# A selective scan beside two other layers: delta's product ahead of the spread and softplus ahead of the decay in the fifth slot

## Chip, cores and metric

The kernel runs on one core of a Trainium2 chip, in one launch. The metric is the device time of that core in microseconds. Before the change it is 28012.72 us, the median of three runs (28011.66 to 28014.21).

The core has five engines that run beside each other and meet through semaphores: TensorE (PE in the profile, with its weight loads shown as PEld), VectorE (DVE), ScalarE (ACT), GpSimd (POOL) and SyncE (SP), which here only issues DMAs. Each has its own queue of instructions.

## What is computed

x has 16 images of 192 channels and 64 x 64 pixels. Four layers follow each other, each added to its input. Each normalises its input by groups of channels first (`_gn`). Layer 0 is a small network per channel, with softplus weights and tanh, of which the kernel does much on TensorE and ScalarE. Layer 1 is a shift in five directions with a product over channels. Layer 2, the scan, is the one that the change is in. Layer 3 is a sum of four depthwise convolutions, a product over channels and a batch norm. Layer 2, cut to what matters (K = 4 directions, N = 16 states, R = 6):

```python
xs = jnp.stack([xf, xt, xf[..., ::-1], xt[..., ::-1]], axis=1)
x_dbl = jnp.einsum('bkdl,kcd->bkcl', xs, x_proj_weight)
dts, Bs, Cs = jnp.split(x_dbl, [R, R + N], axis=2)
dts = jnp.einsum('bkrl,kdr->bkdl', dts, dt_projs_weight)
delta = jax.nn.softplus(dts + dt_projs_bias[None, :, :, None])
A = -jnp.exp(A_logs.astype(jnp.float32)).reshape(K, D, N)
def step(h, inp):
    d, u, Bt, Ct = inp
    dA = jnp.exp(d[..., None] * A)
    h = dA * h + (d * u)[..., None] * Bt[:, :, None, :]
    y = jnp.einsum('bkdn,bkn->bkd', h, Ct)
    return (h, y)
```

The recurrence runs along the 4096 pixels, for each direction, channel and state by itself.

## The kernel before

Two images of 192 channels make 384 rows, that is three tiles of 128 partitions (`NT` = 3); there are 8 such pairs. For each pair `pair` runs `scans` (layer 2) and then `layer3`. Beside the scans of one pair `scans` does the front of the next pair, layers 0 and 1, the projections of layer 2 and their rearrangement: a generator `fr`, of which a little is taken in every step. The front of the first pair runs alone ahead of all, and the last pair's scans have no front beside them.

The scans of a pair are 48 turns (`todo`, index `t`): 3 row tiles, by 4 directions in `ORDER` (1, 3, 0, 2), by 4 stretches of 1024 pixels. A turn has 16 steps, one for each state `n`; `s` counts the steps of a pair. Steps and turns are numbered from 0 here, so the fifth slot of the change is step 4. All engines are given their instructions in program order (`_Engines(tc, True)`), so the loop in `scans` is the order of every queue. A step of the loop issues, in this order:

- SP: the load of C for step s + 2 (`load_c`, two or one of 512 or 256 KB broadcast over partitions); in steps 2, 4 and 6 the loads of later turns' `bp`, `dt` and `xc`.
- VectorE: `product(s)`, du times B in the PSUM tile `pbt`, and `scan(s)`, the recurrence, into an `h` tile in SBUF.
- ScalarE: in `scan(s)`, the copy of the last column of h into `state` for the next turn.
- GpSimd: in `scan(s)`, h times C, in place; in every fourth step (n % 4 == 1) also a DMA that adds the h of the step before to this one.
- ScalarE: `decay(s + 3)`, exp of delta times A into `dA`, preceded by a table load where the active table is another one.
- TensorE: `spread(s + 2)`, which copies row n of B to all partitions of a `pbt` tile (2 matmuls of 512 columns).
- In step 4, the first part of `step_rest(t + 1)`: on TensorE delta's product `v` for the next turn (two halves, four matmul instructions in the trace), on ScalarE softplus of v into `delta`, with a load of the softplus table before. The generator's second part follows in step 8: on GpSimd du = delta times x.
- In all steps but step 5, a share of `fr` (layer 0 keeps step 5 free too): matmuls `p` and tanh, sigmoid or copies on ScalarE for layer 0, matmuls `l_p` for layer 1.
- TensorE: `add_up(s - LATE)`, `LATE` = 4, which adds h to the PSUM tile `ysum` (not for n % 4 == 0); in step 3, ahead of the share of `fr`. Step 3 adds the last h of the turn before and ScalarE copies ysum out to `X` or `Xt`. Step 5 starts this turn's ysum: a turn of direction 0 begins it with eight matmuls, of directions 2 and 3 with four, of direction 1 with none, ahead of the four for h.

`v` and `ysum` share one PSUM buffer (pool `py`, one buffer, one tag). So v waits for the copy of the turn before (step 3), and ysum of step 5 waits for softplus to have read v. `pbt` has two buffers (pool `pb`): the spread of step s + 2 waits for scan s. `dA` has three, `h` eight, `state` is read in the next turn of the same direction. Which buffer of a pool a tile gets is decided when the program is built, by the planner's own estimate of what will be free first, not by rotation alone.

In the profile, all instructions of the scans and of the front beside them have the line of the recording helper, L64; they are told apart by their tiles. `softplus` and `exp` lie in different activation tables (`SOFTPLUS`, `TANH`); layer 0's tanh runs from the exp table or the sigmoid one.

Of the kernel before, what the change touches and what calls it, by code (L numbers as in the profile page):

```python
# [104 lines left out]
def conv_preact_kernel(ctx: ExitStack, tc: tile.TileContext, a: dict):  # L105
# [206 lines left out]
    def image(ap):  # L312
        return ap.rearrange("p (h w) -> p h w", w=HW)
# [468 lines left out]
    def scans(i, o, st3, nxt):  # L782

        E = _Engines(tc, True)
        with ExitStack() as es:
# [22 lines left out]
            T = len(todo)  # L808
# [4 lines left out]
            def seq(t, k, at, n):  # L813


                v = image(t) if k % 2 == 0 else columns(t)
                return v[:, at // HW : (at + n) // HW, :]

            def load_bp(t):
                if t < T:  # L820
                    j, k, at, first = todo[t]
                    bps[t] = two.tile([BP, LC], BF16, name="bp")
                    E.sp.dma_start(out=bps[t], in_=o.bp[k, :, at : at + LC])

            def load_dt(t):
                if t < T:
                    j, k, at, first = todo[t]
                    dts[t] = one.tile([32 + RD, 512], F32, name="dt")
                    src, r = (o.dtp, RD * (k // 2)) if k % 2 else (o.dt, RD * (2 + k // 2))
                    for h in range(2):  # L830
                        E.sp.dma_start(
                            out=dts[t][32 * h : 32 * h + RD, :],
                            in_=src[r : r + RD, at + 512 * h : at + 512 * h + 512],
                        )

            def load_xn(j):
                if j < NT:
                    xns[j] = one.tile([P, L], F32, name="xn")
                    E.sp.dma_start(out=xns[j], in_=row_tiles(o.x2)[:, j, :])

            def norm_xn(j):
                if j < NT:
                    normalise(E.dve, xns[j], xns[j], o.gm, o.rstd, j)

            def load_xc(t):
                if t < T and todo[t][1] == 0:
                    j, k, at, first = todo[t]
                    xcs[t] = one.tile([P, LC], F32, name="xc")
                    E.sp.dma_start(out=xcs[t], in_=row_tiles(o.x2)[:, j, at : at + LC])

            def load_c(s):
                t, n = divmod(s, N)
                j, k, at, first = todo[t]
                cb = cbs[s] = cp.tile([P, LC], F32, name="cb")
                src, row = (o.c, 64 + 16 * k) if k % 2 == 0 else (o.cp, 16 * (k - 1))
                for b, rows in {
                    0: ((0, slice(0, P)),),
                    1: ((0, slice(0, 64)), (1, slice(64, P))),
                    2: ((1, slice(0, P)),),
                }[j]:  # L860
                    r = row + N * b + n
                    E.sp.dma_start(
                        out=cb[rows, :],
                        in_=src[r : r + 1, at : at + LC].to_broadcast([rows.stop - rows.start, LC]),
                    )

            def step_rest(t):


                j, k, at, first = todo[t]  # L870
                dt = dts.pop(t)
                v = py.tile([P, LC], F32, name="v", tag="ysum")
                for h in range(2):
                    rows = slice(32 * h, 32 * h + RD)
                    E.pe.matmul(
                        v[:, 512 * h : 512 * h + 512],
                        dtw[rows, k, j, :],
                        dt[rows, :],
                        start=True,
                        stop=True,  # L880
                    )
                delta = two.tile([P, LC], F32, name="delta")
                E.table(SOFTPLUS)
                E.act.activation(delta, v, AF.Softplus, bias=dtb[:, k, j : j + 1])
                yield
                du = two.tile([P, LC], F32, name="du")
                E.gps.tensor_tensor(image(du), image(delta), seq(xns[j], k, at, LC), ALU.mult)
                made[t] = delta, du

            def decay(s):  # L890
                t, n = divmod(s, N)
                j, k, at, first = todo[t]
                dA = dAs[s] = da.tile([P, LC], F32, name="dA")
                E.table(TANH)
                E.act.activation(dA, made[t][0], AF.Exp, scale=a_neg[:, k, j, n : n + 1])

            def spread(s):
                t, n = divmod(s, N)
                j, k, at, first = todo[t]
                pbt = pbs[s] = pb.tile([P, LC], F32, name="pbt")  # L900
                w = [
                    pick[:, n : n + 1].to_broadcast([BP, P]),
                    pick_mix[:, n, :, :].rearrange("p a b -> p (a b)"),
                    pick[:, N + n : N + n + 1].to_broadcast([BP, P]),
                ][j]
                for c in range(LC // 512):
                    cs = slice(512 * c, 512 * c + 512)
                    E.pe.matmul(pbt[:, cs], w, bps[t][:, cs], start=True, stop=True)

            def product(s):  # L910
                E.dve.tensor_tensor(pbs[s], made[s // N][1], pbs[s], ALU.mult)

            def scan(s):
                t, n = divmod(s, N)
                j, k, at, first = todo[t]
                if (j, k) not in state:
                    state[j, k] = sp_.tile([P, N], F32, name="state")
                dA, pbt, cb = dAs.pop(s), pbs.pop(s), cbs.pop(s)
                back = k >= 2
                flip = slice(None, None, -1) if back else slice(None)  # L920
                h = hs[s] = hp.tile([P, LC], F32, name="h")
                v = state[j, k][:, n : n + 1]
                E.dve.tensor_tensor_scan(
                    h[:, flip], dA[:, flip], pbt[:, flip], 0.0 if first else v, ALU.mult, ALU.add
                )
                E.act.copy(v, h[:, 0:1] if back else h[:, LC - 1 : LC])
                E.gps.tensor_tensor(h, h, cb, ALU.mult)
                if n % 4 == 1:
                    E.gps.dma_start(out=h, in_=hs[s - 1], accum_op=ALU.add)
# [69 lines left out]
            gstep = iter(())  # L999
            for s in range(total):  # L1000
                t, n = divmod(s, N)
                j, k, at, first = todo[t]
                if s + 2 < total:
                    load_c(s + 2)
                if n == 2:
                    load_bp(t + 1)
                if n == 4:
                    load_dt(t + 2)
                if n == 6:
                    load_xc(t + 1)  # L1010
                product(s)
                E.between()
                scan(s)
                if s + 3 < total:
                    decay(s + 3)
                if s + 2 < total:
                    spread(s + 2)
                if (t + 2) % (K * NC_) == 0 and n == 14:
                    load_xn(j + 1)
                if (t + 1) % (K * NC_) == 0 and n == 5:  # L1020
                    norm_xn(j + 1)
                if n > 4:
                    next(fin, None)


                if n == 3:
                    add_up(s - LATE)
                    if s >= LATE and (s - LATE + 1) % (K * NC_ * N) == 0:
                        fin = finish(j - 1)
                elif n == 4:  # L1030
                    gstep = step_rest(t + 1) if t + 1 < T else iter(())
                    next(gstep, None)
                elif n == 8:
                    next(gstep, None)

                if kind == "l0":
                    for _ in range({5: 0}.get(n, 1)):
                        kind = next(fr, None) if kind == "l0" else kind
                elif n != 5:
                    done = 0  # L1040
                    while done < (1.99 if n in (0, 8, 12) else 0.99) and kind != "l0":
                        kind = next(fr, 1)
                        done += kind if isinstance(kind, float) else 1
                if n != 3:
                    add_up(s - LATE)
# [293 lines left out]
```

## Time and profile before

| what | value |
| --- | --- |
| median of three runs | 28012.72 us |
| the profiled execution's own time | 28007.89 us |
| its span | 28006.0 us |
| scans of the first pair | 1210 to 4172 us of the span |
| scans of the last pair | 24486 to 27270 us |
| between two pairs' scans (layer 3) | about 366 us |
| mean granted TensorE clock | 0.912 |

The span runs from the first to the last instruction; 1.9 us of the execution's time lie around it. Within the scans of the first pair, three stages follow each other by what the front does: layer 0 (about 1480 to 2880 us), layer 1 (to about 3500 us) and the projections with their rearrangement, then nothing. Busy time in these stages:

| us of the span | length | PE | DVE | ACT | POOL |
| --- | --- | --- | --- | --- | --- |
| 1210 to 1480 | 270 | 214.70 | 258.73 | 178.60 | 203.94 |
| 2880 to 3500 | 620 | 564.50 | 581.78 | 241.50 | 504.58 |
| 3500 to 4170 | 670 | 497.56 | 609.22 | 338.66 | 490.03 |
| 24486 to 27270 (last pair) | 2784 | 1927.16 | 2667.69 | 1171.76 | 2118.85 |

How to read the lines below: a row of the groups gives the line, the engine, the operation, what it writes and reads, how often, the busy time and mean nanoseconds, and the idle time just before with what ended it. A row of waits gives who waited for whom, with the sum, the number and the longest. In the timeline, the bracket gives the engine's idle time before the instruction and what ended it.

### The profile page before, as it was taken

What the parts mean: (1) busy time and instruction counts of PE and PEld (TensorE: products, weight loads), DVE (VectorE), ACT (ScalarE), POOL (GpSimd) and SP (SyncE); (2) the same over time, 40 slices, a digit from 0 to 9 for tenths busy, and PEclk for the clock granted to TensorE, in tenths of its full rate; (3) what the DMA queues carried; (4) which work ended last, traced back from release to release, by engine and by line L of the source; (5) the groups of instructions that cost most, each with busy time, mean ns of one, the idle gap of its engine ahead of it and who ended that gap; (6) DMA issues with size and microseconds to landing.
All of it is one profiled execution on the core that took longest, in us unless ns stands there. A gap on an engine that the chain in (4) does not pass through costs nothing. (4 is left out here: it accounts for less than half of the span.)

```text
span 28006.0 us, 208082 instructions
## 1 busy us (share of the span) xinstructions
PE 23305.0 (83%) x57140; PEld 9559.7 (34%) x57140; DVE 24196.3 (86%) x15397; ACT 16122.6 (58%) x23044; POOL 20813.2 (74%) x10440
## 2 busy tenths in 40 slices
PE   8799977999689986999779997899968998676663
PEld 4343323333233332333324332333323333222221
DVE  0399988999899998999989998899989999899994
ACT  7388445774468643785548844577446864344433
POOL 2388877887778876888768887788777887677772
PEclk9899988999899998999889998899989999888886
DMA  4489864898568973898748986589856897367765
GB/s 100 132 222 224 215 201 141 220 220 220 157 181 226 220 220 116 220 224 219 212 124 222 224 215 202 141 221 220 219 155 182 226 219 218 114 189 192 192 183 234
DMA packets 2008001, 5448.00 MB, mean 195 GB/s; under 512 B 550392, under 2 KB 550616, under 8 KB 1989424
## 3 DMA queue, kind: packets, MB, share of 16 engines
q1 hardware_dynamic: 1782192, 4578.95, 56.4%
q0 software_dynamic: 221184, 805.40, 15.2%
q10 hardware_dynamic: 3456, 50.33, 0.4%
q8 instruction: 455, 7.45, 0.1%
q14 instruction: 714, 5.85, 0.1%
HBM read 3896.19 MB, written 329.51 MB: 151 GB/s over the span
## 5 line engine op out<-in xcount | busy, mean ns | idle before, releaser
L64 POOL TENSOR_TENSOR h<-h,cb 128x1024 f32<-128x1024 f32 x6144 | 14856.3, 2464 | 4181.8 <-ACT state L64 3664.7
L64 DVE TENSOR_TENSOR_SCAN h<-dA,state,pbt 128x1024 f32<-128x1024 f32 x4608 | 10809.9, 2346 | 675.9 <-ACT dA L64 91.2
L64 PE MATMUL ysum<-h,ident 128*128 128x512 f32 x18432 | 9464.1, 639 | 208.2 <-DMA h<-h 138.6
L64 DVE TENSOR_TENSOR pbt<-du,pbt 128x1024 f32<-128x1024 f32 x6144 | 7434.8, 1210 | 658.0 <-PE pbt L64 619.6
L64 ACT ACTIVATE dA<-delta,t_alog 128x1024 f32<-128x1024 f32 x6144 | 7036.6, 1146 | 4.9
L64 PEld LDWEIGHTS ysum<-h,ident 128*128 128x128 f32 x18432 | 3777.4, 206 | 4520.3 <-issue 3923.8
L64 ACT COPY state<-h 128x1 f32<-128x1 f32 x6144 | 1145.0, 186 | 6401.7 <-DVE h L64 6324.1
L64 PE MATMUL pbt<-bp,pick 96*128 96x512 bf16 x8192 | 2686.3, 412 | 2127.4 <-DVE h L64 2106.9
L64 DVE TENSOR_TENSOR_SCAN h<-dA,pbt 128x1024 f32<-128x1024 f32 x1536 | 3509.1, 2285 | 228.5 <-DMA h<-h 52.6
L64 PE MATMUL p<-t,wts 96*128 96x512 f32 x5376 | 2707.6, 602 | 136.1 <-ACT t L64 135.9
L64 PE MATMUL p<-m,wms 128*96 128x512 f32 (+1 forms) x5376 | 2653.6, 595 | 0.9 <-ACT lu L64 0.3
L64 ACT ACTIVATE t<-p,bias 96x512 f32<-96x512 f32 x2688 | 1809.2, 679 | 1046.2 <-PE p L64 1027.8
L64 PEld LDWEIGHTS <-pick 96*128 96x128 bf16 x8192 | 711.9, 101 | 4920.9 <-DVE h L64 3256.2
L1106 POOL TENSOR_TENSOR l_g<-l_g,l_m 128x1024 f32<-128x1024 f32 x672 | 1615.1, 2405 | 452.3 <-ACT l_g L1102 346.6
L64 PE MATMUL l_p<-l_xp,w1s 128*128 128x512 f32 x3920 | 1844.7, 599 | 3.4 <-POOL l_xp L64 3.3
L1129 DVE SCALAR_TENSOR_TENSOR l_p<-xp,wc,l_p 128x1024 f32<-128x1024 f32 x1248 | 1589.8, 1287 | 262.6 <-PE l_p L1123 231.7
L64 PE MATMUL pbt<-bp,pick_mix 96*128 96x512 bf16 x4096 | 1282.7, 395 | 559.6 <-DVE h L64 555.3
L64 POOL DMA_DIRECT2D h<-h x1536 | 1359.0, 885 | 494.9 <-POOL h L64 427.9
L1111 PE MATMUL l_p<-xp,diag 128*128 128x512 f32 x2688 | 1289.0, 639 | 332.0 <-DVE l_y L1129 281.3
L64 PEld LDWEIGHTS p<-t,wts 96*128 96x128 f32 x5376 | 1007.9, 190 | 1292.6 <-issue 903.8
L64 ACT ACT_TABLE_LOAD x1111 | 1425.4, 1283 | 19.4
L64 POOL TENSOR_TENSOR du<-delta,xn 128x1024 f32<-128x1024 f32 x384 | 1034.5, 2694 | 452.7 <-ACT delta L64 452.7
(219 smaller groups left out, 17750.1 us busy)
## 6 DMA issues: line engine op xcount, KB each, us to landing
cb<-cp_d SPq DMA_DIRECT2D x2048, 512.0 KB
cb<-c_d SPq DMA_DIRECT2D x2048, 512.0 KB
h<-h POOLq DMA_DIRECT2D x1536, 512.0 KB, 7.1
cb<-cp_d SPq DMA_DIRECT2D x2048, 256.0 KB
cb<-c_d SPq DMA_DIRECT2D x2048, 256.0 KB
m<-l_xn SPq DMA_DIRECT2D x3072, 128.0 KB
bp<-bp_d SPq DMA_DIRECT2D x384, 192.0 KB
f0x<-in_x SPq DMA_DIRECT2D x96, 512.0 KB
```

What stands on the lines that cost most here:

```text
L64: return self._tc.keep_in_program_order(call(*args, **kw))
L1106: nc.gpsimd.tensor_tensor(g, g, m, ALU.add)
L1111: nc.tensor.matmul(ps[:, cs], diag[:, j, t, :], window(j, 16 * c + 8 * h, 8, tap), start=(t == 0), stop=False,)
L1129: nc.vector.scalar_tensor_tensor(image(y if tap is TAPS[-1] else ps), window(j, 16 * c, 16, tap), factor(j, tap), image(ps), ALU.mult, ALU ...
```

## The change

In step 4 the first part of `step_rest(t + 1)` is taken right after `scan(s)`, ahead of `decay(s + 3)` and `spread(s + 2)`, and not after them. So on TensorE the four instructions of `v` stand ahead of the spread for step 6, and on ScalarE the load of the softplus table and softplus stand ahead of the decay for step 7. The second part, in step 8, stays. On VectorE and GpSimd no instruction changes its place.

```diff
@@ -1011,6 +1011,11 @@
                 product(s)
                 E.between()
                 scan(s)
+
+
+                if n == 4:
+                    gstep = step_rest(t + 1) if t + 1 < T else iter(())
+                    next(gstep, None)
                 if s + 3 < total:
                     decay(s + 3)
                 if s + 2 < total:
@@ -1021,15 +1026,10 @@
                     norm_xn(j + 1)
                 if n > 4:
                     next(fin, None)
-
-
                 if n == 3:
                     add_up(s - LATE)
                     if s >= LATE and (s - LATE + 1) % (K * NC_ * N) == 0:
                         fin = finish(j - 1)
-                elif n == 4:
-                    gstep = step_rest(t + 1) if t + 1 < T else iter(())
-                    next(gstep, None)
                 elif n == 8:
                     next(gstep, None)
```

## The prediction

> **What bounds the kernel now.** I read the page first: its groups, to see what one step of a scan costs on each engine.
>
> ```profile
> PE 23305.0 (83%) x57140; PEld 9559.7 (34%) x57140; DVE 24196.3 (86%) x15397; ACT 16122.6 (58%) x23044; POOL 20813.2 (74%) x10440
> ...
> L64 DVE TENSOR_TENSOR_SCAN h<-dA,state,pbt 128x1024 f32<-128x1024 f32 x4608 | 10809.9, 2346 | 675.9 <-ACT dA L64 91.2
> L64 DVE TENSOR_TENSOR pbt<-du,pbt 128x1024 f32<-128x1024 f32 x6144 | 7434.8, 1210 | 658.0 <-PE pbt L64 619.6
> L64 ACT ACTIVATE dA<-delta,t_alog 128x1024 f32<-128x1024 f32 x6144 | 7036.6, 1146 | 4.9
> ...
> L64 ACT ACT_TABLE_LOAD x1111 | 1425.4, 1283 | 19.4
> ```
>
> A step on VectorE is product 1.21 + scan 2.35 = 3.56 us, so a turn of 16 steps is 57.0 us at best. Then the list of waits, for VectorE's waits and those that name delta:
>
> ```profile
> DVE pbt L64 <- PE pbt L64: 619.6, 635, 7.7
> ...
> PEld ysum L64 <- ACT delta L64: 344.5, 208, 4.9
> ...
> PE ysum L64 <- ACT delta L64: 236.1, 193, 4.2
> ```
>
> VectorE waits 619.6 us for spreads, and TensorE waits 236.1 us, 193 times, for softplus (the PEld line is the same wait seen by the weight load, not added). Third, busy time in the first pair's layer 0 stage, 1480 to 2880 us (columns: window, length, then busy us of PE, PEld, DVE, ACT, POOL, clock, DMA share, GB/s):
>
> ```profile
> 1480.00:2880.00 1400.00, 1330.13 (x3403) 555.95 (x3404) 1295.81 (x767) 1119.88 (x1658) 1178.99 (x595) 0.98 0.87 222
> ```
>
> TensorE is 95% busy: it paces this stage, and its waits on delta there are 25.5 us in 23. Last, the timeline of turn 9 of that pair (numbered from 0), where the wait is longest. Columns: start, duration, engine, what, and idle before.
>
> ```profile
> 1779.74 1.01 ACT L64 COPY X<-ysum 128x1024 f32<-128x1024 f32 x1 [0.69 <-PE ysum L64]
> ...
> 1784.30 0.18 ACT L64 COPY state<-h 128x1 f32<-128x1 f32 x1
> 1784.49 1.28 ACT L64 ACT_TABLE_LOAD   x1
> 1785.79 1.15 ACT L64 ACTIVATE dA<-delta,t_alog 128x1024 f32<-128x1024 f32 x1
> 1786.95 1.28 ACT L64 ACT_TABLE_LOAD   x1
> 1788.25 1.12 ACT L64 ACTIVATE delta<-v,t_dtb 128x1024 f32<-128x1024 f32 x1
> ```
> ```profile
> 1781.26 0.59 PE L64 MATMUL pbt<-bp,pick 96*128 96x512 bf16 x2
> 1781.78 1.13 PE L64 MATMUL v<-dt,t_dtw 12*128 12x512 f32 x4
> ...
> 1789.42 1.77 PE L64 MATMUL ysum<-xc,ident 128*128 128x512 f32 x2 [4.16 <-ACT delta L64]
> ...
> 1796.37 0.60 PE L64 MATMUL pbt<-bp,pick 96*128 96x512 bf16 x2
> ```
> ```profile
> 1797.00 1.23 DVE L64 TENSOR_TENSOR pbt<-du,pbt 128x1024 f32<-128x1024 f32 x1 [5.78 <-PE pbt L64]
> ```
>
> v was done by 1782.9, but ScalarE, behind with layer 0's tanh, reached step 4's state copy only at 1784.30 and then did a table load, the decay of step 7, another load and softplus. ysum takes the PSUM bank that v held (pool l2_py has one buffer), so TensorE stood 4.16 us, and the spread of step 8 behind ysum came 5.78 us late for VectorE. This is the stall the change reaches.
>
> [...] the load of 1786.95 is followed by softplus at 1788.25. I take 1.28. [...] the spread at 1796.37 stood behind ysum although its buffer was free. [...]
>
> **The change, part by part.** Nothing is computed more or less. In 376 turns (47 of each of 8 pairs) two things move.
>
> ScalarE: load + softplus + load + decay in place of decay + load + softplus (+ load later). Softplus ends 1.15 us earlier, the decay it no longer follows. Where a sigmoid was loaded in step 3, the decay's own load (1784.49) goes too: 2.43 earlier. The built programs hold 1118 loads before and 1097 after; turns 7, 9, 13, 23, 25 of seven pairs lose one, turns 10 and 26 gain one.
>
> TensorE: v's four matmuls (1.06 us from the start of v to what follows: 3007.57 to 3008.63 in turn 29) stand ahead of the spread of step 6 (0.5). v comes no later than before, so SP's dt loads, which wait for v with cb loads behind them, are not held up. du on GpSimd (step 8) gets delta earlier.
>
> Covered: in an unhurried turn state copy, load, softplus, load, decay take 0.19 + 1.28 + 1.11 + 1.28 + 1.15 = 5.0 us from the end of scan 4; scan 7 wants the decay 2 x 3.56 + 1.21 = 8.3 us after it. If ScalarE is over 3.3 us late this cover is gone: turn 9 is 4.0 late, its decay ends at about 1789.35 against scan 7 at 1788.88, 0.5 late, but VectorE waits at step 8 anyway. Likewise v ahead of the spread costs nothing while TensorE is less than about 2 us late there, which holds for turns 0 to 4, 41 to 47 and all of the last pair (no layer work beside it).
>
> Now the first pair, by turn; the other six with a front repeat it within tenths.
> - Turns 9 and 25, wait 4.2 each: 2.43 earlier, 2 x 2.43 = 4.9 us.
> - Turns 8, 11, 37, 39, 40, waits 1.4, 0.5, 1.0, 3.8, 2.8, each with a VectorE stall at step 8: 0.7 (v waits longer for the Xt copy), 0.5, 0.6 (the decay then comes 0.5 late), 1.1, 1.1 = 4.0.
> - Turns 10, 26: softplus earlier by 1.15, but the added load makes the decay of step 8 later by 1.28. I take 0, bounds -0.3 and +1.1 each.
> - h's buffers. The planner hands out the eight buffers by its own estimate of times, so the move shifts them. In the built programs 57 scans of step 9 wait for the GpSimd-issued addition of step 5 before, none after; in 49 more turns step 11 waits for it instead (79 to 128), in the others step 10 takes step 9's place. Turn 24 shows the price:
>
> ```profile
> 2712.08 2.29 DVE L64 TENSOR_TENSOR_SCAN h<-dA,pbt 128x1024 f32<-128x1024 f32 x1 [5.75 <-DMA h<-h]
> ```
>
> One step later the wait is 3.6 shorter, but step 5's state copy moves behind the decay, and with it GpSimd's product and its addition, by about 1.3: 2.3 gained. With turns 25, 36, 38 (1.7 and less, not in every pair): 2.8.
> - The other 16 or so turns of layer 0 with waits of 0.5 to 1.5, together 25.5 - 14.1 (turns 8 to 11, 24 to 26) = 11.4. VectorE mostly isn't held at step 8 there, and TensorE later waits for tanh or a scan again. Bounds 0 and 8; I take 1.5.
> - Spread of step 6 late where TensorE is behind: turns 5, 6, 8, 21, 22, 24, 29, 30, 32, 33, 38, up to 1.06 each, 11.7 at most. In most TensorE paces on at 3.9 us a step and VectorE catches up by step 8. I take -1.0.
>
> Sum 4.9 + 4.0 + 0 + 2.8 + 1.5 - 1.0 = 12.2 us a pair, times 7 = 85; the last pair 0. The profiled execution took 28007.9 (span 28006.0 and 1.9 around it): 27922.9. It lies 4.8 below the median of the runs, 28012.7; on that scale 27928.
>
> **Rivals.**
> 1. The gain is taken back. TensorE saves time on delta and loses it waiting for tanh (p on t: 18.7 us in that window) or a scan (19.9). Only turns 9 and 25 keep theirs, 34 us, and late decays and spreads eat 24 of it: 27998, on the median's scale 28003. For it: VectorE's floor of 57.0 is close to turns of 58 to 61 us. Against: in turns 8, 9, 25, 39 and 40 both engines stand still at once.
> 2. Slower: the spread of step 6. v stands before it in all 376 turns, and where TensorE is behind, the product of step 6 comes 1.06 us late; 11 turns x 1.06 x 7 = 82, if nothing at step 8 gives it back: 28090, or 28095. It decides from the point where VectorE and not TensorE paces the rest of the turn, so that the lag isn't caught up by step 8. For it: turns 29 to 33 have no wait on delta to win. Against: the spreads there are 3.87 apart (3003.17, 3007.05) with TensorE never idle, so VectorE has 0.3 a step to spare.
> 3. More: TensorE paces everything beside layer 0, and each wait on delta counts. Waits over 1.15 lose 1.15 to 2.43, shorter ones vanish: about 160 of the 236.1 us; with 30 of h's buffers 27818, or 27823.
>
> That a transfer hides it is no rival: no load starts later for it but the addition of step 5, counted above.
>
> **How the numbers follow.** The forecast 0.52, rival 1 0.20, rival 2 0.14, rival 3 0.14. A measurement of this kernel tells about 0.2%, 56 us, from no change. Faster by more: nearly all of the forecast, and rival 3: 0.64. Within: rival 1 and the thin end of the forecast: 0.21. Slower: rival 2, and some of rival 1 with a worse handing out of buffers: 0.15. The forecast's own range is 27850 to 27970: the bounds of the small turns (0 to 8 a pair) and of turns 10 and 26. The range that holds 8 in 10 reaches halfway into both outer rivals: 27840 to 28040.
>
> **What would show it.** Right: the wait of ysum on delta falls from 236.1 us to about 90, with 1.7 left in turns 9 and 25; VectorE's wait for spreads falls from 619.6 to about 530, almost all at step 8; table loads 21 fewer; VectorE's wait for the additions, 132.6, falls by some 20, none of it left in step 9. Rival 1: delta's wait falls as much, but p on t or the spread's wait for scans rises. Rival 2: 1 us of wait before the products of step 6 in turns 29 to 33, with turns there longer. I am wrong if the turns of layer 0 other than 8 to 11 and 24 to 26 change by more than a microsecond each, or if the last pair changes at all.

## The result, and the profile after

The changed kernel takes 27866.85 us, the median of five runs (27846.23 to 27874.17); the kernel before, beside it, 28013.31. The ratio is 0.9946, with a 95% interval of 0.9932 to 0.9959: 146 us less, where 85 was forecast. The profiled execution is the fastest of the five, 27846.23 us, with a span of 27844.3 and the clock at 0.912 as before; it lies 161.7 us below the profiled execution of the kernel before, so sums from the two traces come out some 15 us larger than those of the medians.

The page of the changed kernel, engine line and groups:

```profile
PE 23265.5 (84%) x57140; PEld 9539.7 (34%) x57140; DVE 24178.2 (87%) x15397; ACT 16079.1 (58%) x23023; POOL 20784.7 (75%) x10440
...
L64 DVE TENSOR_TENSOR pbt<-du,pbt 128x1024 f32<-128x1024 f32 x6144 | 7429.8, 1209 | 485.4 <-PE pbt L64 444.4
...
L64 ACT ACT_TABLE_LOAD x1090 | 1398.5, 1283 | 19.4
```

21 table loads are gone, as counted. TensorE has the same 57140 matmuls and is busy 39.5 us less (23305.0 before): that is new, and is explained below. The list of waits of the changed kernel (sum in us, number, longest):

```profile
DVE pbt L64 <- PE pbt L64: 444.4, 484, 4.7
...
DVE h L64 <- DMA h<-h: 136.1, 80, 5.5
...
PE v L64 <- ACT Xt L64: 84.1, 79, 2.5
PE v L64 <- ACT X L64: 84.0, 79, 1.1
...
PE ysum L64 <- ACT delta L64: 61.2, 42, 3.3
```

TensorE's wait for softplus fell from 236.1 to 61.2 us, VectorE's for spreads from 619.6 to 444.4. Two rows grew: v, issued before the spread now, waits 84.1 us for the copy to Xt (20.6 before) and 84.0 for the copy to X (none before). Scans wait about as long as before (132.6) for GpSimd-issued additions. By step, worked out from the same traces, VectorE's wait for spreads went from 291.6 to 116.9 us in step 8 and from 14.7 to 66.9 in step 6, that of scans for the additions from 31.5 to 0 in step 9, and up by 33 in steps 1, 2 and 10 together. The product's wait for du, which GpSimd makes from delta, stayed at 25 us, so an earlier du is not where the gain comes from.

Turn 9 of the first pair, in the timeline of the changed kernel:

```profile
1775.61 0.18 ACT L64 COPY state<-h 128x1 f32<-128x1 f32 x1
1775.81 1.28 ACT L64 ACT_TABLE_LOAD   x1
1777.10 1.11 ACT L64 ACTIVATE delta<-v,t_dtb 128x1024 f32<-128x1024 f32 x1
1778.23 1.28 ACT L64 ACT_TABLE_LOAD   x1
1778.27 1.85 PE L64 MATMUL ysum<-xc,ident 128*128 128x512 f32 x2 [1.79 <-ACT delta L64]
...
1780.71 2.35 DVE L64 TENSOR_TENSOR_SCAN h<-dA,state,pbt 128x1024 f32<-128x1024 f32 x1 [0.62 <-ACT dA L64]
...
1785.85 1.23 DVE L64 TENSOR_TENSOR pbt<-du,pbt 128x1024 f32<-128x1024 f32 x1 [2.80 <-PE pbt L64]
```

Between the state copy and softplus there is now one load, and softplus comes before the decay, which follows at 1779.53. So ysum waits 1.79 us and not 4.16, scan 7 waits 0.62 for its late decay, and the product of step 8 waits 2.80 and not 5.78.

### The profile page after: what moved, and what is told of

Its sections match the earlier page's. It is cut to its first block, busy times and chain, and to the rows that moved or that the text cites. A ratio compares the mean times of both kernels' runs of the same rounds, so it can differ in the third digit from the quotient of the medians.

```text
span 27844.3 us, 208067 instructions
## 1 busy us (share of the span) xinstructions
PE 23265.5 (84%) x57140; PEld 9539.7 (34%) x57140; DVE 24178.2 (87%) x15397; ACT 16079.1 (58%) x23023; POOL 20784.7 (75%) x10440
## 5 line engine op out<-in xcount | busy, mean ns | idle before, releaser
L64 DVE TENSOR_TENSOR pbt<-du,pbt 128x1024 f32<-128x1024 f32 x6144 | 7429.8, 1209 | 485.4 <-PE pbt L64 444.4
```

Of the source, the lines that this page charges most:

```text
L64: return self._tc.keep_in_program_order(call(*args, **kw))
```

## The experiments

All ratios are against the kernel before, run on the same chip, with 95% intervals.

**One move at a time.** ScalarE alone: softplus ahead of the decay, v after the spread.

```diff
+                if n == 4:
+                    gstep = step_rest(t + 1) if t + 1 < T else iter(())
+                    next(gstep, None)
                 if s + 3 < total:
                     decay(s + 3)
```

with `spread(s + 2)` moved up in front of these lines, right after `scan(s)`.

> Softplus ahead of the decay on ScalarE, v left behind the spread of step 6 on TensorE. Theory A (the gain is softplus reached earlier in ScalarE's queue; v's place only costs, 43 us of new waits before the products of step 6): at least as fast as the changed kernel, 150 to 200 us below the kernel before, the waits before the products of step 6 gone again. Theory B (v's place on TensorE carries a real part of the gain): 50 to 100 us below the kernel before. Theory C (h's buffers given out anew carry it): about the changed kernel's 146, since the additions of step 5 are again waited for no sooner than step 10.

Measured: 27864.91 us, ratio 0.9946 (0.9934 to 0.9959), not to be told from both moves. TensorE alone: `decay(s + 3)` first, then the first part of `step_rest`, then the spread.

> v ahead of the spread of step 6, softplus left behind the decay. Theory A: 0 to 50 us slower than the kernel before, ysum's wait on delta stays near 236 us. Theory B: 50 to 100 us faster. Theory C: no faster, since the buffers of h are given out as before (57 scans of step 9 wait for the addition of step 5).

Measured: 28019.83 us, ratio 1.0001 (0.9993 to 1.0009); ysum still waits 227.6 us for softplus. So ScalarE's order carries the whole gain. The move on TensorE brings v's waits for the copies (83.5 and 87.9 us in this kernel too) and the late spread of step 6 (93.5 us of waits for spreads at that step here, 14.7 in the kernel before); by itself it wins nothing that can be told from the scatter.

**The buffers of h.** Each h gets its buffer by strict rotation instead of from the planner:

```diff
-            hp = pool("l2h", 8)
+            hp = pool("l2h", 1)
...
-                h = hs[s] = hp.tile([P, LC], F32, name="h")
+                h = hs[s] = hp.tile([P, LC], F32, name="h", tag=f"h{s % 8}")
```

With the order of before:

> The kernel before with the eight h buffers given out in rotation, so that every addition is waited for seven steps after it. Theory A: VectorE's wait for additions, 132.6 us, nearly goes, the kernel gets 50 to 120 us faster, ysum's wait on delta stays at about 236. Theory C: as fast as the changed kernel or faster, 146 us or more below the kernel before.

Measured: 27955.21 us, ratio 0.9979 (0.9970 to 0.9988). With the order of after:

> The changed kernel with the h buffers in rotation, to be set against the kernel before in rotation: with the buffers the same in both, what is left is the two moves alone. Theory A: still 100 to 130 us below it, some 30 us less than the 146 of the change. Theory C: within 40 us of it.

Measured: 27824.79 us, ratio 0.9930 (0.9916 to 0.9944). In both no scan waits for an addition any more. So the planner's choice costs 58.6 us before (28013.8 beside these runs) and 42 after, and with the buffers the same in both, the two moves are worth 130. The other 16 us of the change's 146 would be a luckier hand of buffers, but the scatter of the runs is as large: drawing anew from the recorded times puts the moves at 120 to 144 and the 16 anywhere from 0 to 38.

**Rotation and ScalarE's move alone**, a candidate for the fastest:

> Rotation of h's buffers and softplus ahead of the decay, delta's product left behind the spread, ysum in step 5: a candidate for the fastest. If the move on TensorE is worth nothing: 27805 to 27845, as with both moves (27825). If it is worth something once the buffers rotate: over 27860.

Measured: 27823.45 us, ratio 0.9933 (0.9918 to 0.9948), not to be told from the run with both moves. These two are the fastest kernels of the study.

**A load put back.** In the rotating version of after, the exp table is loaded (with an exp of one column) ahead of softplus, where it is not the active one; that is in turns 9 and 25, 14 loads.

```diff
+                    if E._table != TANH:
+                        E.table(TANH)
+                        E.act.activation(scr, one_c, AF.Exp)
```

> The changed kernel in rotation with the load of the exp table put back ahead of softplus in turns 9 and 25 of seven pairs (and an exp of one column to keep it there). Theory A: these turns lose 1.3 to 1.5 us each, turns 8 to 11 and 24 to 26 together some 3 us a pair against the run without it, nothing elsewhere. Theory D with table loads as its cause: more than that, since every load counts wherever it is.

Measured: 27841.59 us in a single run, 6 us above the profiled run of the kernel without it, which is within the scatter. The wait of ysum on softplus rose from 65.0 to 90.1 us, 1.8 for each load, and turns 8 to 11 grew by 2.8 us a pair, turns 24 to 26 by 0.8. So putting softplus off by a load lengthens the wait and its own turns; what that costs in total can't be told from nothing.

**Taking the wait away by another way.** If the whole gain comes through ysum's wait on softplus, then starting ysum later should win as much, and leave nothing for the moves. With rotating buffers, the ysum of step 5 was issued in step 6, behind the spread:

```diff
                 if s + 2 < total:
                     spread(s + 2)
+                if n == 6:
+                    add_up(s - 1 - LATE)
...
-                if n != 3:
+                if n not in (3, 5):
                     add_up(s - LATE)
```

> The kernel before with h's buffers in rotation, and the first adding into ysum of a turn (step 5) put into step 6, after the spread of step 8. Theory A (softplus matters only because that spread stands behind a ysum that waits for it): most of the two moves' gain without moving softplus, 80 us or more below the kernel before in rotation (27955), VectorE's waits at step 8 nearly gone. Theory D (the gain comes from ScalarE itself, from fewer table loads or from the decays' and tanh's new places): no more than 30 us below it.

> The same put on the changed kernel in rotation. Theory A: the two moves add little to it, under 50 us below the run before with the same late ysum, ysum's wait on delta near 20 us or less. Theory D: 100 us or more below that run, as without the late ysum (130).

> Rotation, late ysum, and of the two moves only softplus ahead of the decay, v behind the spread of step 6. Theory A: as fast as with both moves, or up to 40 us faster, since no product of step 6 is late; the fastest of all, 27790 or less. Theory D: as with both moves.

Measured: 28243.64, 28303.28 and 28223.32 us, ratios 1.0082 (1.0069 to 1.0096), 1.0104 (1.0090 to 1.0118) and 1.0076 (1.0062 to 1.0089), all slower, where 80 us or more of gain had been expected. The wait on softplus was gone (18.1 us in the first of them), and VectorE's waits for spreads at step 8 went from 332.5 us (rotation alone) to 0, but at step 9 they rose from 8.9 to 538.3. The timeline of the first of the three shows it in turn 9 of the last pair, a turn of direction 0:

```profile
25213.12 1.03 PE L64 MATMUL pbt<-bp,pick 96*128 96x512 bf16 x2 [2.60 <-DVE h L64]
25213.94 1.92 PE L64 MATMUL ysum<-xc,ident 128*128 128x512 f32 x2
...
25219.43 3.60 PE L64 MATMUL ysum<-h,ident 128*128 128x512 f32 x8
25222.87 0.60 PE L64 MATMUL pbt<-bp,pick 96*128 96x512 bf16 x2
```
```profile
25223.50 1.23 DVE L64 TENSOR_TENSOR pbt<-du,pbt 128x1024 f32<-128x1024 f32 x1 [3.16 <-PE pbt L64]
```

Two steps' ysum now stand together ahead of the spread of step 9: 16 matmuls in a turn of direction 0, 12 in directions 2 and 3, 8 in direction 1. Here the 16 took 8.93 us, the first two of them 1.92 where the last eight took 3.60, and the product of step 9 waited 3.16; TensorE had stood idle for 2.60 us ahead of the spread in front of them. The wait grows with the burst: of the 538.3 us, 333.4 fell in turns of direction 0, 113.4 and 84.0 in directions 2 and 3, and 7.6 in direction 1. Next, the share of the front was left out of step 6 instead of step 5:

```diff
-                    for _ in range({5: 0}.get(n, 1)):
+                    for _ in range({6: 0}.get(n, 1)):
...
-                elif n != 5:
+                elif n != 6:
```

> Rotation, ysum started in step 6 behind the spread, and the share of the front left out of step 6 rather than of step 5; the order of step 4 as before the change. Theory A (the wait of ysum on softplus is what the change takes away): that wait is gone without the move, and the burst of ysum matmuls no longer stands behind a share of the front, so the time falls to 27870 or less, 80 or more below 27955 (rotation alone), and step 8's wait of VectorE for spreads falls from 338 us to under 200. Rival D (the gain comes from ScalarE's order alone, whatever ysum waits for): 27940 to 27970.

> The same with the changed order of step 4. Theory A: less than 50 us from the run before it, since there is hardly a wait left to take away. Rival D: 100 or more below it, as with ysum in step 5 (130).

> The same with softplus ahead of the decay alone, delta's product behind the spread. Theory A: within 30 us of the run before it. Rival D: also within 30, both 100 or more below the first run of these three.

Measured: 28322.28, 28405.66 and 28382.88 us, ratios 1.0111 (1.0094 to 1.0128), 1.0142 (1.0126 to 1.0157) and 1.0134 (1.0119 to 1.0149). The waits of step 9 stayed, at 508.5 us in the first of the three, so they don't need a share of the front within the burst. That of step 8 was 190.0 (332.5 with rotation alone, which the expectation has as 338), and with step 6 emptied instead of step 5 TensorE's waits for tanh rose from 143.4 us to 423.5. The wait on softplus was 2.7 us in the first of these three, and the moves gained nothing there (83 and 61 us lost); without the emptied step 6, both moves had lost 60 and ScalarE's alone had won 20. That fits the theory that the gain needs the wait, but doesn't show it: these kernels are held up at another place. What is shown is that ScalarE's order makes the gain; that it does so through ysum's wait is read from the traces.

## Why the prediction was right, and too small

The time fell as forecast, and inside the range; the forecast's own gain, 85 us, is 0.6 of what came, and the measured time lies nearer to rival 3's number (27823, 44 us off) than to the forecast's (27928, 61 off). In turns 9 and 25 the mechanism was the one forecast. But the prediction had also said that it would be wrong if the other turns of layer 0 changed by more than a microsecond each, or the last pair at all, and both came: turns 5, 6, 7, 13, 14, 21 and 22 are 1.2 to 2.4 us shorter in the mean of seven pairs, and the last pair is 3.5 longer. The prediction's terms beside the measured lengths of the turns, as gains in us a pair, mean of the seven pairs with a front:

| term of the sum | forecast | after against before | the two moves alone (both with rotation) |
| --- | --- | --- | --- |
| turns 9, 25 | 4.9 | 7.9 | 6.6 |
| turns 8, 11, 37, 39, 40 | 4.0 | 3.6 | 5.2 |
| turns 10, 26 | 0 | 1.6 | 1.2 |
| turns 24, 36, 38 (buffers) | 2.8 | 3.1 | -0.6 |
| other turns of layer 0: 5 to 7, 12 to 18, 21 to 23 | 1.5 | 9.7 | 6.6 |
| late spread, turns 27 to 33 | -1.0 (with turns of the rows above) | -2.5 | -3.1 |
| all other turns | 0 | -0.2 | 0.1 |
| sum | 12.2 | 23.0 | 15.9 |

Each column comes from one execution of each kernel. They make 158 and 108 us in all, where the medians give 146 and 130, so the two sums are known to some 3 us a pair, and small differences between the columns mean nothing.

- Right: softplus 2.43 us earlier in turns 9 and 25 (ysum's wait is 2.37 shorter in the timeline above), the decay of step 7 then half a microsecond late (0.62), step 8 as the place, 21 loads, no scan of step 9 left waiting for an addition, the move on TensorE worth nothing but a late spread of step 6, and turn 24, where the scans' waits for additions fell from 23.2 to 7.8 us over all pairs and the turn gained 2.8 us a pair more than with rotation (2.3 forecast for it). That the buffers in all come to 16 us, near the 20 forecast, is no proof of the path: the waits for additions did not fall by 20 but rose from 132.6 to 136.1, and the 16 has the scatter given above.
- The term that was mis-sized is the one of the other turns of layer 0: "VectorE mostly isn't held at step 8 there, and TensorE later waits for tanh or a scan again. Bounds 0 and 8; I take 1.5." It was 9.7, or 6.6 for the moves alone (8.7 and 7.0 where only ScalarE's order was changed). TensorE mostly did not wait again later. The waits in turns 5 to 26 of the first pair, before:

```profile
DVE pbt L64 <- PE pbt L64: 44.9, 52, 7.6
...
PE ysum L64 <- ACT delta L64: 25.0, 22, 4.2
...
PE p L64 <- ACT t L64: 18.7, 12, 1.8
...
PE pbt L64 <- DVE h L64: 14.3, 13, 3.9
```

and after:

```profile
PE p L64 <- ACT t L64: 17.4, 16, 2.4
DVE pbt L64 <- PE pbt L64: 16.7, 31, 2.8
...
PE pbt L64 <- DVE h L64: 14.8, 17, 5.3
...
PE ysum L64 <- ACT delta L64: 4.5, 3, 1.8
```

20.5 us of waits on softplus went, and those on tanh (18.7 to 17.4) and on scans (14.3 to 14.8) stayed. This pair is a good one. In turns 5 to 26 of all seven pairs 138.8 us of waits on softplus went (170.2 to 31.4) and those on tanh stayed (128.6 to 124.1), but those on scans rose from 94.1 to 125.3; TensorE's idle time in all fell by 94.3. So about two thirds of it stayed gone, and a third came back, where the forecast had nearly all of it come back outside the large stalls. One way can be followed in turn 14 of the first pair: its wait of 0.49 us at ysum was gone, TensorE still waited 1.70 for tanh near the turn's end, since tanh itself waits for TensorE's p and moves with it, and VectorE's stall at the product of step 14 fell from 1.06 to 0.21. So a delay in step 5 seems to have come out at that product. In the forecast I had looked for the price at step 8 only.
- A second part of it I had not in the sum at all: the same matmuls took less time. The windows of turns 5 to 26 of the first pair (window, length, then busy us of PE, PEld, DVE, ACT, POOL, clock, DMA share, GB/s), before and after:

```profile
1519.16:2862.16 1343.00, 1279.25 (x3270) 534.92 (x3269) 1240.65 (x735) 1079.06 (x1596) 1128.68 (x571) 0.98 0.87 222
```
```profile
1517.86:2828.02 1310.16, 1266.34 (x3269) 530.07 (x3268) 1238.73 (x735) 1072.14 (x1592) 1125.55 (x570) 0.99 0.90 227
```

Of 32.8 us that this stretch is shorter, TensorE's busy time is 12.9 and its idle time 19.9. Over turns 5 to 26 of all seven pairs it is 69.4 and 94.3, of 163.8 us; between the two rotations 49.8 and 76.2, of 126.0. In these turns the trace has the granted clock at one half for 337.9 us before and for 218.4 after; over the whole span it hardly changed (4936 and 4922), so it fell by 119.5 where TensorE paces and rose by some 106 elsewhere. Turn 22 shows how. Before:

```profile
2561.22 1.02 PE L64 MATMUL p<-t,wts 96*128 96x512 f32 x2
2563.95 1.48 PE L64 MATMUL p<-t,wts 96*128 96x512 f32 x2 [1.70 <-ACT t L64]
2565.22 3.27 PE L64 MATMUL ysum<-h,ident 128*128 128x512 f32 x4
```

After:

```profile
2543.71 1.02 PE L64 MATMUL p<-t,wts 96*128 96x512 f32 x2
2545.77 1.13 PE L64 MATMUL p<-t,wts 96*128 96x512 f32 x2 [1.04 <-ACT t L64]
2546.74 1.88 PE L64 MATMUL ysum<-h,ident 128*128 128x512 f32 x4
```

After a wait of 1.70 us four matmuls of ysum took 3.27 us, after one of 1.04 the usual 1.88. So in this turn, before the change, TensorE's wait was followed by ysum matmuls that took 1.39 us longer, in a stretch for which the trace has the granted clock at 0.50 (the last section has its windows). That the wait was the cause is my reading of the traces. The division of the gain between this and the waits themselves is read from the traces and was not tried by itself.
- Turns 9 and 25 gave 7.9 and not 4.9: the first pair's turn 9 shortened by 2.5 us as worked out, but its turn 25 by 5.8, and turn 9 of the seven pairs by 2.5 to 5.2; "the other six with a front repeat it within tenths" doesn't hold. By pair the gain was 16.4 to 33.6 us, so one pair can't stand for all.
- Wrong, and small: the wait for additions moved to other steps; the last pair is 3.5 us longer and not unchanged, 3.2 also with ScalarE's move alone (VectorE waits 2.3 us more for spreads there and 1.5 more for an addition; why is open); turn 16 is 2.0 longer, where VectorE waits longer for GpSimd's sum of X and Xt at the change of row tile (two waits of 2.0 at most before, three of 3.4 at most after, in the first pair).
- Of the rivals, the third had the better view of layer 0 (every wait of TensorE counts), but its 190 us were too many for the whole kernel. The measured time stayed inside the forecast's own range, 17 us from its lower end, though the term of the other turns of layer 0 passed its upper bound of 8 in the full change; that is partly luck.

## What to carry to other kernels

Where one engine paces a stage, don't count on its later waits to absorb a short stall of it early in a turn. Here two thirds of what went did not come back; in the turn that was followed, the later wait was for work that the engine feeds itself, and moved along with it. Look at every wait of the pacing engine, not only at those behind which the second engine stands still at once. And before crediting a gain to an order, take the hand of buffers apart from it: here a rotation that changed no order was worth 58.6 us, and together with one move on ScalarE gave one of the two fastest kernels.

## What the runs showed of the hardware

That TensorE would run at half rate after short waits was not expected. In both kernels, neighbouring matmuls of 512 columns into the same tile start 0.43 us apart where the trace has the granted clock at 1.00, and 0.85 where it has it at 0.50 (medians). Three neighbouring windows of turn 22 in the kernel before, the second of which holds the slow ysum (columns as above; the clock is the last but two):

```profile
2561.16:2564.57 3.41, 1.71 (x6) 0.61 (x5) 3.21 (x3) 3.40 (x6) 3.11 (x3) 1.00 1.04 204
2564.57:2567.99 3.42, 3.42 (x6) 1.30 (x5) 2.97 (x2) 2.96 (x5) 3.42 (x3) 0.50 1.10 242
2567.99:2571.40 3.41, 3.41 (x10) 1.41 (x9) 2.34 (x2) 0.72 (x1) 1.69 (x1) 1.00 1.02 243
```

Turn 22 is not alone. The span of the kernel before, from 1.37 ms on, was cut into windows like these three, 3.413 us long, with the changes of the recorded clock on the cuts (all 1349 fit, to within 0.05 us). Of the 658 windows at a clock of 1.00 in which TensorE was busy for less than half, 602 were followed by one at 0.50; of the 5756 busier ones, 66 were. In the changed kernel it is 577 of 622 and 70 of 5751. Half a window is where I divided them, not a limit that the traces show, and single cases differ: turn 22's wait of 1.70 us made its window 50% busy, and the next was at 0.50; turn 14's, as long, also lay within one window, 50% busy, and no slow stretch followed. In the changed kernel turn 14's wait of 1.70 fell to two windows as 0.48 and 1.22, and none followed either. TensorE's ends in these traces are modelled, so the shares are rough. What makes the clock change is not shown by these runs; they show how often its drop came behind idle time.
